# Two-layer relational graph network: single-row transfers on SyncE in layer 2 and on ScalarE in layer 1, and layer 2's root product made in layer 1

## The chip, the core and the metric

The kernel runs on one core of a Trainium2 chip. The time of a run is the core's device time for one execution, in microseconds, and the metric is the median of several runs. The engines of the core work side by side: TensorE (PE in the profile; its weight loads are PEld), VectorE (DVE), ScalarE (ACT), GpSimd (POOL) and SyncE (SP). Each engine takes its instructions in program order, and waits on semaphores for what the others make. A DMA is issued by an instruction in an engine's queue and then runs by itself.

## What is computed

A graph has N = 12500 nodes with 128 features each, and 200000 edges with a source, a destination and one of R = 8 relations. The edges come sorted by destination. Two layers of a relational graph convolution run, each with a residual, and a layer norm ends it. Cut to what matters:

```python
def _rgcn_conv(x, src, dst, et, basis, comp, root, bias):
    W = jnp.einsum('rb,bio->rio', comp, basis)          # 8 matrices 128x128
    xw = jnp.einsum('ni,rio->nro', x, W)
    msgs = xw[src, et]
    seg = dst * N_REL + et
    summed = segment_sum(msgs, seg)
    cnt = segment_sum(ones, seg)
    mean = summed / jnp.maximum(cnt, 1.0)[:, None]
    agg = mean.reshape(N_NODES, N_REL, HIDDEN).sum(axis=1)
    return agg + x @ root + bias

h = x
for l in range(2):
    h = relu(_rgcn_conv(h, src, dst, et, basis[l], comp[l], root[l], bias[l])) + h
return _layernorm(x + h)
```

The part that the change moves is `x @ root + bias` of the second layer, where x is the output h of the first.

## The kernel before

`ordered_path` records every operation in a `Plan`, engine by engine, which afterwards writes out the semaphore waits. So the order on each engine is the order in which the code calls the helpers, and the helpers' lines are what the profile shows: `load` (L701) for every ordinary DMA, `copy` (L704) for ScalarE's copies, `pe`, `vec`, `act` and `pool` for the rest. A DMA issued "on SyncE" or "on ScalarE" stands in that engine's queue among its other instructions.

**Tiles.** The sorted edges are cut into 1563 tiles of 128, and eight tiles make a quad (NQ = 196 quads). Nodes are cut into 98 blocks of 128; a block takes about two quads of edges.

**Rows of the sources.** Each tile needs the 128 rows of its sources, 512 bytes each, at addresses that only the edge list knows. GpSimd gathers them with one indirect DMA per tile (`gather`, L806), into a ring of seven buffers of one quad each (`rows_r`, AHEAD = 5 quads ahead). For some tiles the rows come another way, by single-row transfers: `SINGLES` lists them, as an engine, a layer and a range of tiles. `single_lists` writes the tile's byte offsets to DRAM once. `single_rows` then has the engine load 32 offsets into its registers (L755) and issue one DMA per row (L759), 128 rows in eight chunks of 16, spread over as many steps as lie between two such tiles; every other chunk needs a new register load. The rows land in one of two buffers `hw_`; a tile's last chunk is issued some three quads ahead of its use. Before the change there are 24 such tiles, all of layer 1 and all on SyncE: every 56th from tile 191.

**Layer 1** goes quad by quad, in steps of a loop over o. TensorE forms the means per destination slot and relation from the gathered rows and one-hot tiles of VectorE (`means`, L1364, into two banks `s`); ScalarE copies them to `sT` (`take_means`); TensorE multiplies by the eight relation matrices (`product`, L1396) and puts the result at its node's place (`place`, L1427, with layer 1's root product at L1429); VectorE adds carry and bias, relu and residual (`finish`, L1448, L1452, L1472), which gives a block of hT. From each block `table` (L1495) makes the block's 8 x 128 rows of y = h W_r for layer 2; ScalarE copies them from `pt` or `ct` to `y_row` and stores them to `y_d` in DRAM (`stores`). Tables are made from step TABLE = 50 on, not all of them at once: between steps 94 and 162 (SORT - 2 to SORT + NR + 4) one per step at most, before and after up to two. On ScalarE, `batch(o)` sets the order of a step: the copies that are left from the step before, `ys`, the two `sT` copies, then the stores, then the single rows that ScalarE has, if any.

**Layer 2** gathers rows of `y_d`, which are already multiplied by the relation matrix. Most quads q under 192 that are not in `ROUTED` are summed by slot (`slot_sums`, L2026) from gathered rows; 62 of the quads, every third (7, 10, ... 190), are "routed": TensorE picks their values out of transposed copies of y in SBUF (`pick_rows` L1918, `add_up` L1938, `relate` L1958), with only one gather each for what is left over (`gather_left`). The index lists `lo_d` and `sc_d` of each routed quad, the block hT (`h_d`, `open_block`), x and the output go over SyncE's queue. `place_sums` (L2059) places a quad's sums into the block's accumulator `s`, and in the quad that opens a block adds the root product there (L2063) from the block of `h_d`. `finish` adds the carry of the block before and takes up the next carry with the bias (L1452). The last four quads are added by `add_rows` (L2083).

In layer 2, then, GpSimd has eight gathers per ordinary quad and one per routed quad: 51 in nine quads.

Of the kernel before, what the change touches and what calls it, by code (L numbers as in the profile page):

```python
# [8 lines left out]
F32 = mybir.dt.float32  # L9
# [421 lines left out]
def ordered_path(  # L431
# [80 lines left out]
    RC, RL = 16, 32  # L512
    SINGLES = [("SP", 0, range(191, NQ * Q - 80, 56))]
    SINGLE = {(l, t): (i, k) for i, (_, l, ts) in enumerate(SINGLES) for k, t in enumerate(ts)}
# [16 lines left out]
    w_d = dram.tile([L, R * D, D], F32, name="w_d")  # L531
    h_d = dram.tile([NT, D, P], F32, name="h_d")

    idx = keep([P, B * P], I32, "idx")
# [676 lines left out]
    def rows_of(j):  # L1211
        return min(P, N - j * P)
# [222 lines left out]
    def finish(l, k, apart=False):  # L1435
# [3 lines left out]
        def first_step():  # L1439
            a, ac = acc[k] if apart and k + 1 < NT else acc.pop(k)  # L1440
            emits, reads, cells = [], [ac, ("bias_t", l)], []
            if k >= 0:
                vs[k] = a, ac
            if (l, k) == (1, NT - 1):
                return
            if k >= 0:
                t, c = carry.pop(k)
                emits.append(lambda: nc.vector.tensor_add(a[:, :n], a[:, :n], t[:, :n]))  # L1448
                reads.append(c)
            if k + 1 < NT and not apart:  # L1450
                nt, ncell = carry[k + 1] = carry_r.take()
                emits.append(lambda: nc.vector.tensor_scalar(nt, a[:, P:], bias_t[:, l:l + 1], None, op0=ALU.add))  # L1452
                cells.append(ncell)

            vec(in_turn(emits), reads, cells)
# [29 lines left out]
    def table(j):  # L1485
# [552 lines left out]
    def place_sums(q, k, opens, last):  # L2038
        t, c = pl.pop(q)
        o, oc = ys.pop(q)  # L2040
        a, ac = acc[k]
        root_in = opens and k >= 0
        reads = [c, oc]
        m = NW if q in ROUTED else P
        if root_in:
            ht, hc = hb[k]
            reads += [hc, ("w", 1, R)]
        more = []
# [9 lines left out]
        def emit():  # L2058
            ins = nc.tensor.matmul(a, o[:m], t[:m], start=opens, stop=last and not root_in and not more)  # L2059
            for rows_m, dm_m in more:  # L2060
                ins = nc.tensor.matmul(a, rows_m, dm_m, start=False, stop=last and not root_in)  # L2061
            if root_in:
                ins = nc.tensor.matmul(a[:, :rows_of(k)], w_sb[:, 1, R, :], ht[:, :rows_of(k)], start=False, stop=last)  # L2063
            return ins
# [4 lines left out]
    def add_rows(q, k, opens, last, between_last=None):  # L2069
# [3 lines left out]
        n = in_quad(q)  # L2073
        root_in = opens and k >= 0
        more = []
        if root_in:
            ht, hc = hb[k][0][:, :rows_of(k)], hb[k][1]
            more += [hc, ("w", 1, R)]

        def some(i0, i1):  # L2080
            def emit():
                for i in range(i0, i1):
                    ins = nc.tensor.matmul(a, t[:, i, :], d[:, i, :],  # L2083
                                           start=(opens and i == 0), stop=(last and i == n - 1))
                    if i == 0 and root_in:
                        nc.tensor.matmul(a[:, :rows_of(k)], w_sb[:, 1, R, :], ht, start=False, stop=False)
                return ins

            return emit

        if q == NQ - 2:
            for h in range(2):
                pe(some(4 * h, 4 * h + 4), [c + (h,)] + dc + more, [ac, ("done", 1)])
        elif q == NQ - 1:
# [10 lines left out]
        else:  # L2105
            pe(some(0, n), [c + (0,), c + (1,)] + dc + more, [ac, ("done", 1)])
        plan.mark("PE")
# [207 lines left out]
    for o in range(NG - 3):  # L2315
# [95 lines left out]
    batch(None)  # L2411
    end()
    placed(g - 4)
    product(g - 3)
# [35 lines left out]
    for _, b in halves:  # L2450
        b()

    for q in range(AHEAD):
# [152 lines left out]
```

## Time and profile before

The profile is one execution, taken by the hardware profiler. Its page has, in this order: busy time by engine, the span in 40 slices, DMA queues, the chain of work that ended last, groups of instructions by line, and DMA issues. The views of the trace used beside it are windows (busy time of each engine in a stretch of the span), the timeline of a stretch (start, duration, engine, line, operation, and in brackets the idle time before it with what ended it), and groups by line. A name with q (SPq, ACTq) is the queue of an engine that issues DMAs, whose time isn't counted as busy.

| | |
|---|---|
| runs | 3383.34, 3384.41, 3385.06 us; median 3384.41 |
| the profiled execution's own time | 3385.05 us |
| its span in the trace | 3383.1 us |
| mean granted clock of TensorE | 0.911 |
| moved by DMA | 289.03 MB in 171649 packets, 85 GB/s |
| HBM read / written | 218.35 MB / 65.70 MB |

```profile
## 2 busy tenths in 40 slices
PE   6777667877667777777776739999999999999995
DVE  6665454463367888888333238888888888888884
ACT  1211112222122222222222211111111111111110
POOL 7777777777777777777777777777777777777775
PEclk8999879888888888888988879999999999999997
```

Each digit is a slice of 84.6 us. Layer 1 fills the first 24 slices, the seam between the layers lies in the 24th, and layer 2 fills the rest.

### The profile page before, as it was taken

To read this page: it belongs to the slowest core of one execution; us is meant where nothing else is said; L and a number is where in the kernel's file an instruction comes from. 1 tells how busy PE (TensorE), PEld (TensorE's weight loads), DVE (VectorE), ACT (ScalarE), POOL (GpSimd) and SP (SyncE) were. 2 spreads that over 40 slices of the span, in tenths; PEclk is the share of its full clock that TensorE was granted. 3 is DMA by queue.
4 is the path that set the end of the run, shared out by engine and by line. 5 is a ranking of instruction groups with operands and counts; after the bars stand their busy time and mean duration, and the time that the engine had idled before them with its cause. 6 is when DMAs were issued, how large, how long until landed. Compare 5 with 4: busy or idle time off the path is not lost.

```text
span 3383.1 us, 73915 instructions
## 1 busy us (share of the span) xinstructions
PE 2766.1 (82%) x27537; PEld 2228.2 (66%) x27537; DVE 2270.8 (67%) x6302; ACT 644.9 (19%) x1627; POOL 2547.9 (75%) x2677
## 2 busy tenths in 40 slices
PE   6777667877667777777776739999999999999995
PEld 4565565656566666766565627777777777777774
DVE  6665454463367888888333238888888888888884
ACT  1211112222122222222222211111111111111110
POOL 7777777777777777777777777777777777777775
PEclk8999879888888888888988879999999999999997
DMA  4242223443322232222333232233223322333222
GB/s 138 56 59 64 57 77 113 132 130 95 89 82 81 75 89 76 82 77 82 115 105 89 88 101 73 72 84 85 78 78 84 84 78 78 84 85 82 78 78 61
DMA packets 171649, 289.03 MB, mean 85 GB/s; under 512 B 66163, under 2 KB 102813, under 8 KB 171285
## 3 DMA queue, kind: packets, MB, share of 16 engines
q0 software_dynamic: 85408, 175.09, 20.3%
q1 hardware_dynamic: 47146, 50.19, 5.0%
q10 hardware_dynamic: 38731, 58.99, 4.9%
q8 instruction: 218, 3.57, 0.5%
q14 instruction: 146, 1.20, 0.1%
HBM read 218.35 MB, written 65.70 MB: 84 GB/s over the span
## 4 chain that ended last, share of the span: by engine, by line
PE 43%; POOL 40%; issue 13%; DVE 2%; DMA 2%; ACT 1%; POOLq 0%; ACTq 0%; SPq 0%; DVEq 0%
POOL rows L806 40%; PE pt L1918 11%; PE y L1938 9%; PE po L1938 7%; PE po L1958 3%; PE s L2059 3%; PE ct L2026 2%; PE s L1364 2%; PE y L1396 1%; DMA rows<-in_x_dram,idx 1%; PE s L2061 1%; DVE dm L1270 1%; PE s L2063 1%; DVE arena L999 1%; PE pt L1495 0%
## 5 line engine op out<-in xcount | busy, mean ns | idle before, releaser
L806 POOL DMA_INDIRECT rows<-in_x_dram,idx x1539 | 1476.8, 960 | 471.3 <-issue 463.5
L806 POOL DMA_INDIRECT rows<-y_d,idy x1067 | 1010.4, 947 | 325.1 <-issue 316.6
L1364 PE MATMUL s<-dm,rows 128*128 128x128 f32 x3078 | 531.6, 344 | 379.6 <-DMA rows<-in_x_dram,idx 351.8
L1364 PEld LDWEIGHTS s<-dm,rows 128*128 128x128 f32 x3078 | 495.2, 252 | 441.1 <-issue 228.1
L1270 DVE TENSOR_SCALAR dm<-cols,kr,w 128x128 f32<-128x128 f16 x1563 | 525.1, 400 | 194.7 <-PE pt L1495 54.8
L1396 PE MATMUL y<-w_sb,sT 128*128 128x128 f32 x3136 | 438.6, 299 | 46.4 <-ACT sT L704 46.4
L1396 PEld LDWEIGHTS y<-w_sb,sT 128*128 128x128 f32 x3136 | 424.6, 217 | 56.4 <-ACT sT L704 55.2
L1918 PE MATMUL pt<-arena,dm 128*32 128x128 f32 x12152 | 391.3, 275 | 2.8 <-DVE dm L1868 2.1
L704 ACT ACTIVATE sT<-s 128x512 f32<-128x512 f32 x391 | 212.3, 594 | 824.8 <-PE s L1364 824.8
L1918 PEld LDWEIGHTS pt<-arena,dm 128*32 128x32 f32 x12152 | 324.6, 110 | 55.2 <-issue 43.0
L1938 PE MATMUL y<-arena,dm 128*128 128x304 f32 x620 | 229.6, 452 | 35.1 <-DVE arena L1885 35.1
L1229 DVE TENSOR_SCALAR sT<-cols,kr,w 128x32 f32<-128x32 f16 x1040 | 238.1, 300 | 7.4 <-PE s L2063 7.3
L1868 DVE TENSOR_TENSOR dm<-arena,cols 128x768 f32<-128x768 f16 x248 | 231.3, 933 | 4.1 <-DMA dm<-sc_d 3.7
L1448 DVE TENSOR_TENSOR po<-po,carry 128x128 f32<-128x128 f32 x98 | 28.8, 294 | 296.9 <-PE pt L1495 104.2
L1938 PE MATMUL po<-arena,dm 128*128 128x304 f32 x620 | 210.3, 421 | 0.0
L704 ACT ACTIVATE dm<-pt 128x256 f32<-128x256 f32 x248 | 95.4, 385 | 578.2 <-PE pt L1918 533.6
L1495 PE MATMUL pt<-w_sb,arena 128*128 128x512 f32 (+1 forms) x326 | 174.5, 618 | 26.3 <-ACT y_row L704 14.9
L704 ACT ACTIVATE y_row<-pt 128x512 f32<-128x512 f32 x165 | 98.5, 597 | 417.8 <-PE pt L1495 153.3
L1938 PEld LDWEIGHTS y<-arena,dm 128*128 128x128 f32 x620 | 102.9, 189 | 88.4 <-DVE arena L1885 35.3
L1885 DVE TENSOR_SCALAR arena<-cols,comp_sb 128x608 f32<-128x608 f16 x155 | 134.9, 902 | 36.1 <-DMA arena<-y_d,arena 36.0
L1938 PEld LDWEIGHTS po<-arena,dm 128*128 128x128 f32 x620 | 118.4, 191 | 41.3 <-issue 0.7
L1885 DVE TENSOR_SCALAR arena<-cols,sel 128x608 f32<-128x608 f16 x155 | 134.8, 902 | 0.0
(327 smaller groups left out, 3583.5 us busy)
## 6 DMA issues: line engine op xcount, KB each, us to landing
hw_SP<-in_x_dram SPq DMA_DIRECT2D x3072, 0.5 KB
y_d<-y_row ACTq DMA_DIRECT2D x96, 512.0 KB
rows<-in_x_dram,idx POOLq DMA_INDIRECT x1539
rows<-y_d,idy POOLq DMA_INDIRECT x1067
arena<-lo_d SPq DMA_DIRECT2D x62, 256.0 KB
x_g<-in_x_dram SPq DMA_DIRECT2D x24, 512.0 KB
h_d<-arena ACTq DMA_DIRECT2D x96, 64.0 KB
out_dram<-x_g SPq DMA_DIRECT2D x12, 512.0 KB
```

The lines of the kernel that those rows point to most:

```text
L704: act(lambda: nc.scalar.activation(out_t, in_t, AF.Copy), reads, writes)
L806: ins.append(nc.gpsimd.indirect_dma_start(out=t[:, i - q * Q, :], out_offset=None, in_=table_t, in_offset=bass.IndirectOffsetOnAxis(ap=ids ...
L1229: vec(in_turn([lambda i=i: nc.vector.tensor_scalar(t[:, i, :], cols[:, :2 * K], kr[:, i0 + i:i0 + i + 1], w[:, i0 + i:i0 + i + 1], op0=ALU ...
L1270: emits.append(lambda i=i: nc.vector.tensor_scalar(t[:, i - q * Q, :wide], cols[:, :wide], ids[:, i:i + 1], w[:, i:i + 1], op0=ALU.is_equa ...
L1364: last = nc.tensor.matmul(s_b[i // 4][0][:, i % 4, :], t[:, i, :] if one is None else one[0], d[:, i, :], start=True, stop=True)
L1396: last = nc.tensor.matmul(y[:m], t[:, r, :nt, :].rearrange("p t k -> p (t k)"), w_sb[:, 0, r, :], start=(r == 0), stop=(r == R - 1))
L1495: pe(lambda: nc.tensor.matmul(hb[:n].rearrange("p r d -> p (r d)"), hT[:, j * P:j * P + n], w_sb[:, 1, k * H:(k + 1) * H, :].rearrange("p ...
L1868: emits = [lambda: nc.vector.tensor_tensor(o[:, :3 * n].rearrange("p (j c) -> p j c", j=3), bits[:, None, u * n:(u + 1) * n].to_broadcast( ...
L1885: vec(lambda v=v, o=o: nc.vector.tensor_scalar(o, segs_p, sg[:, v:v + 1], sg[:, NTL + v:NTL + v + 1], op0=ALU.is_equal, op1=ALU.mult), ["n ...
L1918: last = nc.tensor.matmul(b[k * CAP:(k + 1) * CAP, x, :], o[:n, c:c + CAP], hT[:n, j * P:(j + 1) * P], start=jj == 0, stop=jj == SIZE[g] - 1)
L1938: last = nc.tensor.matmul(b.rearrange("p t d -> p (t d)")[:, :SEG], g[:, x * P:(x + 1) * P], o[:, k * SEG:(k + 1) * SEG], start=v == 0, st ...
L1958: pe(in_turn([lambda r=r: nc.tensor.matmul(b[:NW, 0, :], t_s[:, r * NW:(r + 1) * NW], w_sb[:, 1, r, :], start=r == 0, stop=r == R - 1) for ...
```

## The change

Three things are changed.

1. `SINGLES` gets two entries. SyncE brings 21 tiles of layer 2 (every 72nd from tile 95, so one in nine quads, none of them in a routed quad), and ScalarE 12 tiles of layer 1 (every 104th from tile 244, one in 13 quads). GpSimd no longer gathers these 33 tiles. The address list of each entry is made by `single_lists` at the step that `LISTED` gives for its layer.
2. A new function `rooting(k)` makes layer 2's root product for block k in layer 1, one step or more after the block's hT is there: one matmul of TensorE into a free part of the `y` bank, one ScalarE instruction that adds the bias and puts it in one of two buffers `hr`, and a store to `hr_d` on ScalarE's queue.
3. In layer 2 `open_block` loads `hr_d[k]` beside `h_d[k]`, on SyncE; `finish` makes the carry of block k+1 by adding `hr` in place of the bias; the root matmul goes from `place_sums` and `add_rows`. The last block, 97, keeps its own root product.

```diff
-    SINGLES = [("SP", 0, range(191, NQ * Q - 80, 56))]
+    SINGLES = [("SP", 0, range(191, NQ * Q - 80, 56)), ("SP", 1, range(95, (NQ - 4) * Q, 72)), ("ACT", 0, range(244, NQ * Q - 80, 104))]
...
+    hr_d = dram.tile([NT, D, P], F32, name="hr_d")
...
+    hr_r = Ring(const, 2, [P, P], F32, "hr")
+    hr, rooted = {}, []
...
             if k + 1 < NT and not apart:
                 nt, ncell = carry[k + 1] = carry_r.take()
-                emits.append(lambda: nc.vector.tensor_scalar(nt, a[:, P:], bias_t[:, l:l + 1], None, op0=ALU.add))
+                if l == 1 and k + 1 < NT - 1:
+                    rt, rc = hr.pop(k + 1)
+                    emits.append(lambda: nc.vector.tensor_add(nt, a[:, P:], rt))
+                    reads.append(rc)
+                else:
+                    emits.append(lambda: nc.vector.tensor_scalar(nt, a[:, P:], bias_t[:, l:l + 1], None, op0=ALU.add))
...
+    def rooting(k):
+        n = rows_of(k)
+        b, bc = y_full[0][:, 1, :n], y_full[1]
+        t, c = hr_r.take()
+        pe(lambda: nc.tensor.matmul(b, w_sb[:, 1, R, :], hT[:, k * P:k * P + n], start=True, stop=True),
+           [("h", k), ("w", 1, R)], [bc])
+        plan.mark("PE")
+        act(lambda: nc.scalar.activation(t[:, :n], b, AF.Identity, bias=bias_t[:, 1:2]), [bc, ("bias_t", 1)], [c])
+        plan.mark("ACT")
+        stores.append(lambda: load(hr_d[k][:, :n], t[:, :n], [c], [("hr_d", k)], "ACT"))
...
         load(t[:, :n], h_d[k][:, :n], [("h_d", k)], new(c))
         hb[k] = t, c
+        if k < NT - 1:
+            t, c = hr[k] = hr_r.take()
+            load(t[:, :n], hr_d[k][:, :n], [("hr_d", k)], [c])
...
         def emit():
-            ins = nc.tensor.matmul(a, o[:m], t[:m], start=opens, stop=last and not root_in and not more)
+            ins = nc.tensor.matmul(a, o[:m], t[:m], start=opens, stop=last and not more)
             for rows_m, dm_m in more:
-                ins = nc.tensor.matmul(a, rows_m, dm_m, start=False, stop=last and not root_in)
-            if root_in:
-                ins = nc.tensor.matmul(a[:, :rows_of(k)], w_sb[:, 1, R, :], ht[:, :rows_of(k)], start=False, stop=last)
+                ins = nc.tensor.matmul(a, rows_m, dm_m, start=False, stop=last)
             return ins
...
             if k >= 0:
                 stores.append(lambda k=k: load(h_d[k][:, :rows_of(k)], hT[:, k * P:k * P + rows_of(k)], [("h", k)],
                                                [("h_d", k)], "ACT"))
+                if k < NT - 1:
+                    rooted.append(k)
                 tables.extend(table(k))
...
         for step in behind:
             pe(*step)
             plan.mark("PE")
         behind.clear()
+        if rooted:
+            rooting(rooted.pop(0))
         if len(tables) > 4 and (TABLE <= o < SORT - 2 or o >= SORT + NR + 4):
```

How this changes the order on ScalarE, in a step of layer 1 that makes two tables. Before (the number behind a name is a buffer's, and `y_row` stands for the rows of y that go to `y_d`):

```order
L704 ACTIVATE ys_120<-y 128x128
L704 ACTIVATE sT_113<-s_136 128x4x8x16
L704 ACTIVATE sT_113<-s_137 128x4x8x16
L701 DMA y_d<-y_row_127 128x1024
L704 ACTIVATE y_row_128<-pt 128x512
L704 ACTIVATE y_row_127<-pt 128x512
L704 ACTIVATE y_row_127<-ct 128x512
L704 ACTIVATE ys_121<-y 128x128
```

and a like step of the changed kernel that has a chunk of a single-row tile (`hw_ACT`) and a root product (`hr`); lines are those of the changed kernel:

```order
L708 ACTIVATE ys_119<-y 128x128
L708 ACTIVATE sT_114<-s_137 128x4x8x16
L708 ACTIVATE sT_114<-s_138 128x4x8x16
L705 DMA y_d<-y_row_128 128x1024
L759 TENSOR_LOAD off_d_165
L763 DMA hw_ACT_158<-in_x_dram 1x512 x16
L1535 ACTIVATE hr_154<-y,bias_t 128x128
L708 ACTIVATE y_row_129<-pt 128x512
L708 ACTIVATE y_row_128<-pt 128x512
L708 ACTIVATE y_row_128<-ct 128x512
L708 ACTIVATE ys_120<-y 128x128
```

The register load, the sixteen row transfers and the root product's copy now stand between the store and the three copies out of `pt` and `ct`.

On SyncE, in layer 2, the loads of the routed quads' lists (`lo_d`, `sc_d`) and of the blocks (`h_d`) were alone:

```order
L701 DMA arena<-lo_d 128x1024
L701 DMA id_k<-h_d 128x128
L701 DMA dm<-sc_d 16x128
L701 DMA id_r<-h_d 128x128
L701 DMA arena<-lo_d 128x1024
L701 DMA jmp<-h_d 128x128
L701 DMA dm<-sc_d 16x128
```

In the changed kernel the same stretch of the queue reads:

```order
L705 DMA arena<-lo_d 128x1024
L705 DMA id_k<-h_d 128x128
L705 DMA hr_155<-hr_d 128x128
L759 TENSOR_LOAD off_d_164
L763 DMA hw_SP_157<-y_d 1x512 x32
L705 DMA dm<-sc_d 16x128
L705 DMA id_r<-h_d 128x128
L705 DMA hr_154<-hr_d 128x128
L759 TENSOR_LOAD off_d_164
L763 DMA hw_SP_157<-y_d 1x512 x16
L705 DMA arena<-lo_d 128x1024
L763 DMA hw_SP_157<-y_d 1x512 x16
```

Each block load is followed by one of `hr_d`, and chunks of 16 rows, with a register load before every other one, stand between the block loads and the lists.

More of the change, by code (lines that the diff above doesn't have):

```diff
@@ L2041, in place_sums @@
         a, ac = acc[k]
-        root_in = opens and k >= 0
         reads = [c, oc]
         m = NW if q in ROUTED else P
-        if root_in:
-            ht, hc = hb[k]
-            reads += [hc, ("w", 1, R)]
         more = []
@@ L2058, in emit @@
         def emit():
-            ins = nc.tensor.matmul(a, o[:m], t[:m], start=opens, stop=last and not root_in and not more)
+            ins = nc.tensor.matmul(a, o[:m], t[:m], start=opens, stop=last and not more)
             for rows_m, dm_m in more:
-                ins = nc.tensor.matmul(a, rows_m, dm_m, start=False, stop=last and not root_in)
-            if root_in:
-                ins = nc.tensor.matmul(a[:, :rows_of(k)], w_sb[:, 1, R, :], ht[:, :rows_of(k)], start=False, stop=last)
+                ins = nc.tensor.matmul(a, rows_m, dm_m, start=False, stop=last)
             return ins
@@ L2073, in add_rows @@
         n = in_quad(q)
[L2074 to L2078, printed above, removed]
         def some(i0, i1):
@@ L2084, in emit @@
                                            start=(opens and i == 0), stop=(last and i == n - 1))
-                    if i == 0 and root_in:
-                        nc.tensor.matmul(a[:, :rows_of(k)], w_sb[:, 1, R, :], ht, start=False, stop=False)
                 return ins
@@ L2092, in add_rows @@
             for h in range(2):
-                pe(some(4 * h, 4 * h + 4), [c + (h,)] + dc + more, [ac, ("done", 1)])
+                pe(some(4 * h, 4 * h + 4), [c + (h,)] + dc, [ac, ("done", 1)])
         elif q == NQ - 1:
@@ L2105, in add_rows @@
         else:
-            pe(some(0, n), [c + (0,), c + (1,)] + dc + more, [ac, ("done", 1)])
+            pe(some(0, n), [c + (0,), c + (1,)] + dc, [ac, ("done", 1)])
         plan.mark("PE")
@@ L2412, in ordered_path @@
     end()
+    while rooted:
+        rooting(rooted.pop(0))
     placed(g - 4)
@@ L2451, in ordered_path @@
         b()
+    while rooted:
+        rooting(rooted.pop(0))
+    rooting(NT - 2)
+    for step in stores:
+        step()
+    stores.clear()
     for q in range(AHEAD):
```

## The prediction

> **What bounds the kernel now.** I read the page's head, its chain and its costliest groups first, then the stages as windows.
>
> ```profile
> span 3383.1 us, 73915 instructions
> PE 2766.1 (82%) x27537; PEld 2228.2 (66%) x27537; DVE 2270.8 (67%) x6302; ACT 644.9 (19%) x1627; POOL 2547.9 (75%) x2677
> PE 43%; POOL 40%; issue 13%; DVE 2%; DMA 2%; ACT 1%; POOLq 0%; ACTq 0%; SPq 0%; DVEq 0%
> L806 POOL DMA_INDIRECT rows<-in_x_dram,idx x1539 | 1476.8, 960 | 471.3 <-issue 463.5
> L806 POOL DMA_INDIRECT rows<-y_d,idy x1067 | 1010.4, 947 | 325.1 <-issue 316.6
> ```
>
> GpSimd looks like a 75% engine and is a full one. Its gathers take 0.945 us, each behind 0.3 us of issue, and nearly none of its idle time has another releaser: one gather every 1.25 us, from the first microsecond to the last stage, without a stop between the layers.
>
> ```profile
> core 0: us, PE busy (x) PEld busy (x) DVE busy (x) ACT busy (x) POOL busy (x), PEclk, DMA share, GB/s
> 560.00:960.00 400.00, 298.21 (x1700) 241.84 (x1701) 179.99 (x547) 100.91 (x206) 303.32 (x318) 0.88 0.36 110
> 1600.00:1780.00 180.00, 132.98 (x753) 106.40 (x751) 65.92 (x203) 47.06 (x99) 136.08 (x145) 0.90 0.35 108
> 2030.00:3300.00 1270.00, 1264.51 (x17659) 965.64 (x17658) 1085.03 (x2768) 193.33 (x561) 960.39 (x1017) 1.00 0.29 80
> ```
>
> In layer 1 (the first two stages shown) TensorE and ScalarE have room and GpSimd has none. In layer 2 TensorE is full as well. Which of the two sets the end there shows in its last stretch:
>
> ```profile
> L2063 PE MATMUL s<-id_r,w_sb x64: 272/275/422, 2040.1 to 3324.2; 128*128 128x128 f32 x64
> 3333.56 1.10 PE L2026 MATMUL ct<-rows,sT 128*32 128x128 f32 x16 [8.90 <-DMA rows<-y_d,idy]
> 3342.45 6.72 PE L2083 MATMUL s<-dm,rows 128*128 128x256 f32 x16 [4.50 <-DMA rows<-y_d,idy]
> ```
>
> The first row times the blocks: block 1 opens at 2040.1 and block 94 at 3324.2, so 93 blocks take 1284.1 us, 13.81 per block of two quads, 62.1 per nine quads. In nine quads GpSimd makes 6 x 8 + 3 = 51 gathers, 63.75 us. TensorE starts layer 2 late, catches up by 1.6 us in nine quads, and at 3333 waits 8.9 us for rows: GpSimd's queue sets the end, TensorE comes a hair behind it.
>
> **The change part by part.** *Gathers.* 12 leave GpSimd in layer 1 and 21 in layer 2: 33 x 1.25 = 41.2 us, 15.0 and 26.2. That is the gain if everything else keeps up. TensorE would: the root product is two instructions, and sixteen such take 1.8 us back to back (1006.06, below), so a product is 0.22 us, 21 us over the 95 that leave layer 2's blocks, or 1.0 per nine quads. In layer 1 that work meets an engine with 26% idle.
>
> ```profile
> L1448 DVE TENSOR_TENSOR po<-po,carry 128x128 f32<-128x128 f32 x98 | 28.8, 294 | 296.9 <-PE pt L1495 104.2
> L1452 DVE TENSOR_SCALAR carry<-po,bias_t 128x128 f32<-128x128 f32 x97 | 33.1, 341 | 0.0
> ```
>
> The carry turns from a scalar form of 0.34 into a tensor-tensor add, of which a like one takes 0.29: nothing.
>
> *What pays for the gathers* is the queue of another engine, and for that I read the transfers of before.
>
> ```profile
> L755 SPq TENSOR_LOAD <-off_d x96: 3512/3756/4675, 190.3 to 1758.5; - x96
> 640.67 21.45 SPq L759 DMA_DIRECT2D hw_SP<-in_x_dram  x52
> 1011.92 7.98 SPq L759 DMA_DIRECT2D hw_SP<-in_x_dram  x25
> 2502.64 0.32 SPq L701 DMA_DIRECT2D arena<-lo_d  x1
> 2503.00 0.43 SPq L701 DMA_DIRECT2D id_k<-h_d  x1
> ```
>
> A row costs 7.98/25 = 0.32 us of its engine's queue in a clean stretch. The 52 rows of 21.45 us have one register load of 3.76 among them: 0.34. A tile of 128 rows has four loads: at 0.34, which I take as the longer stretch, 15.0 + 43.5 = 58.6 us; at 0.32 and the shortest load 55.
>
> *SyncE in layer 2.* It has nine quads per tile. In them stand, beside the tile, 3 loads of `lo_d`, 3 of `sc_d`, 4.5 of `h_d`, the 4.5 new ones of `hr_d`, and one of x or out: 16 at 0.32 to 0.43, 5.1 to 6.9. Together **64.5 us, against 62.5 that GpSimd then needs (50 gathers) and 61.1 of TensorE**. SyncE becomes the slowest. Behind its rows, in order, wait the block loads, for which VectorE's carry and residual wait. Against the pace of before that is 2.4 us per nine quads, and 93 blocks are 20.7 times nine: +49. A tile's last chunk is issued three quads ahead of its use, so 20.7 us of lag cost nothing: +28. At the end TensorE no longer waits 8.9 us for GpSimd, which is ahead by then: -9. Layer 2: **+19**. The bounds: at 55 + 5.1 = 60.1 SyncE is hidden and the layer gains 1.25 us per nine quads on GpSimd's pace, about -26; with none of the lag forgiven +49.
>
> *ScalarE in layer 1.* A tile goes in eight chunks of 16 rows, each after the step's `sT` copies, and every other one behind a register load: 5.4 or 9.2 us in 8 of 13 steps. Here is a step of the first stage with tables:
>
> ```profile
> 649.79 2.05 PE L1364 MATMUL s<-dm,rows 128*128 128x128 f32 x16 [2.65 <-DMA rows<-in_x_dram,idx]
> 651.88 0.60 ACT L704 ACTIVATE sT<-s 128x512 f32<-128x512 f32 x1 [3.45 <-PE s L1364]
> 651.88 0.33 ACTq L701 DMA_DIRECT2D y_d<-y_row  x1
> 652.37 0.59 ACT L704 ACTIVATE sT<-s 128x512 f32<-128x512 f32 x1
> 654.52 0.60 ACT L704 ACTIVATE y_row<-pt 128x512 f32<-128x512 f32 x1 [1.56 <-PE pt L1495]
> 655.17 1.12 PE L1495 MATMUL pt<-w_sb,arena 128*128 128x512 f32 x2 [0.26 <-ACT y_row L704]
> 656.14 1.02 PE L1495 MATMUL ct<-w_sb,arena 128*128 128x512 f32 x2
> 657.20 0.60 ACT L704 ACTIVATE y_row<-pt 128x512 f32<-128x512 f32 x1 [2.07 <-PE ct L1495]
> 658.75 1.83 PE L1364 MATMUL s<-dm,rows 128*128 128x128 f32 x14 [1.59 <-DMA rows<-in_x_dram,idx]
> 660.84 0.60 ACT L704 ACTIVATE sT<-s 128x512 f32<-128x512 f32 x1 [2.39 <-PE s L1364]
> 658.17 0.28 ACT L704 ACTIVATE ys<-y 128x128 f32<-128x128 f32 x1
> 1000.99 0.44 ACTq L701 DMA_DIRECT2D lo_d<-arena  x1
> ```
>
> ScalarE frees `pt` at 654.52, and TensorE's second table waits for it. The queue hands out the store at 651.88, so the chunk would run from 652.2 to 657.6, or to 661.4 with a load; with the `hr` copy (0.28, as `ys`) that `y_row` starts 3.4 or 7.2 us late, and all of TensorE behind it with it: table, second table in `ct`, the next means. Without a chunk and with rows at hand, TensorE could go on at 657.1, and the next `sT` would come 2.1 us after (658.75 to 660.84): a step of 7.3. With one it is 10.7 or 14.5. Thirteen steps: 5 x 7.3 + 4 x 10.7 + 4 x 14.5 = 137, and 1.5 for seven root products, **against 13 x 10.0 - 1.25 = 128.8 of GpSimd**. To that comes the clock:
>
> ```profile
> 1006.06 1.80 PE L1364 MATMUL s<-dm,rows 128*128 128x128 f32 x14 [1.22 <-ACT arena L704]
> 1016.56 3.75 PE L1364 MATMUL s<-dm,rows 128*128 128x128 f32 x16 [4.36 <-DMA rows<-in_x_dram,idx]
> ```
>
> After a wait of 4.4 us the means take 3.75 instead of 1.8 to 2.05, and the granted clock of the stage is 0.88. A TensorE that waits 3 to 7 us for ScalarE pays about 1.8 us more: in the four loaded steps and half the others, 11 us. The excess is 21 us in 13 quads. The Trainium skill's TensorE: Matmul & The Clock Gate (HAM oscillation) says that an idle stretch of more than some 3.4 us puts the array back to half clock; the two rows agree. Without the clock the excess would be 10.
>
> Tables stand in 560 to 960 and from 1600 until the last chunk near 1750, some 53 quads or 4.1 times thirteen: 86 us of lag. (Between them, and before, steps have one table or none; I take their lag as constant.) The ring of seven row tiles lets GpSimd run on for five and a half quads, 55 us; the rest, 31 us, it stands still. With the 15.0 gained, layer 1: **+16**. Bounds: -15 with no stall; with rows at 0.44, the longer of ScalarE's own issues (`lo_d`), 13 us more in each thirteen, +69. That the lag left drains before the layer ends I take from the 7.3 us step: 2.7 us a quad over the 22 quads behind the last chunk.
>
> *The layers' seam.* The last root product stands behind the last tables, so `y_d` is not later, and GpSimd ends first there:
>
> ```profile
> 1949.39 0.95 POOL L806 DMA_INDIRECT rows<-in_x_dram,idx  x1 [0.30 <-issue]
> 2026.40 1.86 DVE L1885 TENSOR_SCALAR arena<-cols,comp_sb 128x608 f32<-128x608 f16 x2 [36.02 <-DMA arena<-y_d,arena]
> ```
>
> The layer's last gather is out at 1949, and VectorE's first selection behind the seam waits 36.0 us for rows until 2026: a shift of layer 1 goes through whole, and the last products, 22 quads of 0.22 late at most, cost nothing. The address lists add two small loads: nothing.
>
> **The sum**, against the profiled execution's own time, 3385.05 us (span 3383.1, 1.95 around it; the median of the three runs, 3384.41, is 0.6 less): 3385 + 16 + 19 = **3420**.
>
> **The rivals.** *Both queues keep up.* Mechanism: the chunk lies in the time that ScalarE stands idle (in 560 to 960 it is busy 101 of 400 us), TensorE catches up in the five free steps, and SyncE at 0.32 a row is inside 62.5. It decides at a mean excess of zero: thirteen steps under 128.8 us, a ScalarE row of 0.25 or a second table not held. Then GpSimd's 33 gathers are the whole effect: 3385 - 41 = 3344. The Trainium skill's Perfetto Trace Analysis (DMA Optimizations) has it so: where descriptor generation is what keeps an engine solid, balance the DMAs over the engines that can issue. GpSimd here is such an engine, and the trace agrees about it; that the others have the room is what the 58.6 us per tile speak against. *SyncE keeps up, ScalarE doesn't:* 16 - 26, 3375. *ScalarE keeps up, SyncE doesn't:* -15 + 19, 3389. *Both worse:* rows at 0.44 on ScalarE, or the steps between the tables lagging too: 69 + 19, 3473.
>
> **How the numbers follow.** The forecast of 3420 (3395 to 3445) 0.42; both keep up, 0.14; only SyncE, 0.15; only ScalarE, 0.12; both worse, 0.17. The range, 3345 to 3490, leaves out the lower half of the first rival (0.07) and the upper part of the last (0.08). Within 0.2% (about what a measurement of this kernel can tell from no change) means 3378 to 3391: faster by more has the first rival and most of the second, 0.25; within, the rest of it and half of the third, 0.10; slower 0.65.
>
> **What would show it.** GpSimd's gathers of layer 1 with releasers on TensorE, some 30 us, and its last one at about 1965 instead of 1949; TensorE waiting for `y_row` copies by more than 3 us in 560 to 960, at a clock under 0.88; SyncE's issues without a gap in layer 2, blocks at 14.2 us instead of 13.8, and waits of slot sums for `hw_SP` or of VectorE for `hr`. Wrong it is if GpSimd never waits, or if blocks come at 13.6.

## The result and the profile after

| | median | runs | |
|---|---|---|---|
| before | 3383.95 us | 5, 3383.15 to 3385.06 | |
| changed | 3480.24 us | 5, 3473.26 to 3487.11 | ratio 1.0287, interval 1.0271 to 1.0303 |

The change costs 96 us. The forecast was 3420, 36 us slower, with a range up to 3490. The direction and the range held, the size did not. The profiled execution took 3477.2 us.

The page's head and its chain of work, with the two groups of gathers:

```profile
span 3475.3 us, 83036 instructions
PE 2732.8 (79%) x27537; PEld 2164.6 (62%) x27537; DVE 2264.0 (65%) x6304; ACT 674.1 (19%) x1724; POOL 2508.3 (72%) x2644
PE 34%; SPq 17%; ACTq 16%; DVE 11%; issue 10%; POOL 5%; DMA 4%; ACT 4%; DVEq 0%; POOLq 0%
L810 POOL DMA_INDIRECT rows<-in_x_dram,idx x1527 | 1457.4, 954 | 529.7 <-issue 454.2 <-PE s L1368 69.3 <-DMA arena<-in_dst_dram 2.3
L810 POOL DMA_INDIRECT rows<-y_d,idy x1046 | 990.3, 947 | 391.0 <-issue 306.2 <-PE ct L2049 75.9 <-PE s L2080 3.4
```

The chain has moved: GpSimd held 40% of it and now 5%, and two queues of DMA issues, SyncE's and ScalarE's, hold 33%. GpSimd now stops, 69 us in layer 1 and 76 us in layer 2, both times for a row buffer that TensorE has not yet released.

Where the 92 us of span come from is read from the first and last start of the gathers, here before and after (views of the tile `rows`):

```profile
L806 POOL DMA_INDIRECT rows<-in_x_dram,idx x1539: 940/945/1986, 4.6 to 1949.4; - x193
L806 POOL DMA_INDIRECT rows<-y_d,idy x1067: 940/945/1817, 1950.6 to 3363.7; - x178
```

```profile
L810 POOL DMA_INDIRECT rows<-in_x_dram,idx x1527: 938/944/1883, 4.5 to 1988.3; - x191
L810 POOL DMA_INDIRECT rows<-y_d,idy x1046: 938/944/2599, 1989.6 to 3448.4; - x175
```

Layer 1 ends its gathers at 1988.3 instead of 1949.4: **+38.9**. Layer 2's take 1458.8 us instead of 1413.1: +45.7. The stretch behind the last gather, 19.4 before, is 26.9 now: +7.5. So **layer 2 and the end cost 53 us**.

**Layer 1.** The queue and the engines in a step before any table is made (timelines of ScalarE and of TensorE):

```profile
224.47 1.08 ACT L708 ACTIVATE sT<-s 128x512 f32<-128x512 f32 x2
228.67 5.34 ACTq L763 DMA_DIRECT2D hw_ACT<-in_x_dram  x16
234.05 0.28 ACT L708 ACTIVATE ys<-y 128x128 f32<-128x128 f32 x1 [8.50 <-issue]
235.21 0.37 ACT L1535 ACTIVATE hr<-y,bias_t 128x128 f32<-128x128 f32 x1 [0.88 <-PE y L1532]
```

```profile
234.38 0.80 PE L1532 MATMUL y<-arena,w_sb 128*128 128x128 f32 x2 [4.99 <-ACT ys L708]
235.82 3.41 PE L1368 MATMUL s<-dm,rows 128*128 128x128 f32 x16
239.06 1.95 PE L1400 MATMUL y<-w_sb,sT 128*128 128x128 f32 x16
```

```profile
core 0: us, PE busy (x), PEclk, DMA share, GB/s
229.40:232.00 2.60, 0.00 (x0) 1.00 0.20 52
232.10:238.80 6.70, 4.42 (x18) 0.50 0.23 61
```

`ys`, the copy out of the `y` bank, stands behind a register load and the chunk: ScalarE computes nothing for 8.5 us ahead of it. The root product writes a part of the same bank, which the plan tracks as one piece, so it waits 5.0 us for that copy, and everything of TensorE behind it waits too: place, and the next means. Those then take 3.41 us where the sixteen products behind them take 1.95: the granted clock is 0.50 from 232.1 to 238.8 (last view), and 1.00 before and behind that stretch. The Trainium skill's TensorE: Matmul & The Clock Gate (HAM oscillation) warns of idle gaps of more than some 3.4 us, behind which the next matmuls start at the throttled clock. The trace agrees for this wait of 5.0 us; here the lower clock set in 2.6 us after TensorE's last matmul. Such waits add up (waits of TensorE from 200 to 560 us, before and after):

```profile
PE s L1364 <- DMA rows<-in_x_dram,idx: 50.5, 24, 4.1
PE y L1396 <- ACT sT L704: 30.8, 27, 1.2
```

```profile
PE y L1400 <- ACT sT L708: 41.0, 15, 7.4
PE y L1532 <- ACT ys L708: 35.0, 12, 7.2
PE pt L961 <- ACT arena L708: 34.6, 4, 11.5
```

How late TensorE is when the first table begins shows in the first start of `table`, here before and after:

```profile
L1495 PE MATMUL pt<-w_sb,arena x326: 592/592/1222, 517.9 to 1962.9; 128*128 128x512 f32 x162, 128*84 128x512 f32 x1
L1504 PE MATMUL pt<-w_sb,arena x326: 592/595/1223, 553.4 to 2001.6; 128*128 128x512 f32 x162, 128*84 128x512 f32 x1
```

It is 35.5 us late there, before any table is made.

**Layer 2.** SyncE's rows, a stretch of its queue, and the last chunk of the first tile and of the last:

```profile
L763 SPq DMA_DIRECT2D hw_SP<-y_d x2688: 227/228/724, 2029.3 to 3430.5; - x192
2599.69 0.36 SPq L705 DMA_DIRECT2D jmp<-h_d  x1
2600.10 0.42 SPq L705 DMA_DIRECT2D hr<-hr_d  x1
2600.62 5.11 SPq L763 DMA_DIRECT2D hw_SP<-y_d  x16
2605.83 0.32 SPq L705 DMA_DIRECT2D dm<-sc_d  x1
2609.91 5.09 SPq L763 DMA_DIRECT2D hw_SP<-y_d  x16
2106.18 5.12 SPq L763 DMA_DIRECT2D hw_SP<-y_d  x16
3425.66 5.12 SPq L763 DMA_DIRECT2D hw_SP<-y_d  x16
```

The waits of VectorE and SyncE from 2126 to 3396, SyncE's longest from 2029 to 2126, and its longest before the change, from 2030 to 3300:

```profile
DVE s L1452 <- DMA hr<-hr_d: 188.6, 57, 6.5
SPq L705 <- PE pt L1941: 1.6, 5, 0.6
SPq L705 <- PE po L1919: 21.6, 1, 21.6
SPq L701 <- PE po L1896: 552.9, 59, 44.6
```

From 2126 on SyncE never rests: its longest sum of waits is 1.6 us of 1270 (the hole before 2609.91 is a register load). Before the change one releaser alone held it 553 us. The rows of 21 tiles take from 2029.3 to 3430.5. Among them is one stop of 21.6 us, in the first tile; from the last chunk of the first tile to that of the last, 20 tiles take 1319.5 us, **66.0 us each**, for nine quads. An `hr` load takes 0.52 us of the queue (2600.10 to 2600.62). VectorE's add waits for it in 57 blocks. At the end it is the same queue (timelines of TensorE and of GpSimd):

```profile
3432.21 0.87 PE L2049 MATMUL ct<-rows,sT 128*32 128x128 f32 x11 [17.22 <-DMA hw_SP<-y_d]
3407.15 0.94 POOL L810 DMA_INDIRECT rows<-y_d,idy  x1 [43.26 <-PE ct L2049]
```

TensorE waits 17 us for the last tile that SyncE brings, whose last row is issued at 3430.5. It waits for no gathered rows any more: GpSimd had been so far ahead that it stood still for 43 us for a buffer, so that the 26 us which 21 gathers less save are lost in waiting.

### The profile page after: what moved, and what is told of

The parts are those of the page before. It is cut to its first block, busy times and chain, and to the rows that moved or that the text cites. A ratio compares the mean times of both kernels' runs of the same rounds, so it can differ in the third digit from the quotient of the medians.

```text
span 3475.3 us, 83036 instructions
## 1 busy us (share of the span) xinstructions
PE 2732.8 (79%) x27537; PEld 2164.6 (62%) x27537; DVE 2264.0 (65%) x6304; ACT 674.1 (19%) x1724; POOL 2508.3 (72%) x2644
## 4 chain that ended last, share of the span: by engine, by line
PE 34%; SPq 17%; ACTq 16%; DVE 11%; issue 10%; POOL 5%; DMA 4%; ACT 4%; DVEq 0%; POOLq 0%
ACTq L763 11%; SPq L763 10%; PE s L1368 7%; SPq L759 5%; POOL rows L810 5%; PE y L1400 5%; PE pt L1941 4%; ACTq L759 4%; PE y L1961 3%; PE pt L1504 3%; PE po L1961 3%; SPq L705 2%; DVE dm L1274 2%; DMA hr<-hr_d 1%; ACT sT L708 1%
## 5 line engine op out<-in xcount | busy, mean ns | idle before, releaser
L810 POOL DMA_INDIRECT rows<-in_x_dram,idx x1527 | 1457.4, 954 | 529.7 <-issue 454.2
L810 POOL DMA_INDIRECT rows<-y_d,idy x1046 | 990.3, 947 | 391.0 <-issue 306.2
L1274 DVE TENSOR_SCALAR dm<-cols,kr,w 128x128 f32<-128x128 f16 x1563 | 526.2, 403 | 130.8 <-PE ct L1504 62.1
L1368 PEld LDWEIGHTS s<-dm,rows 128*128 128x128 f32 x3054 | 407.4, 211 | 78.3 <-issue 73.6
L1368 PE MATMUL s<-dm,rows 128*128 128x128 f32 x3054 | 422.1, 296 | 35.7 <-DMA hw_SP<-in_x_dram 17.7
L1941 PE MATMUL pt<-arena,dm 128*32 128x128 f32 x12152 | 404.6, 281 | 57.0 <-DVE dm L1891 36.9
L1941 PEld LDWEIGHTS pt<-arena,dm 128*32 128x32 f32 x12152 | 336.1, 112 | 123.5 <-issue 116.6
L1504 PE MATMUL pt<-w_sb,arena 128*128 128x512 f32 (+1 forms) x326 | 197.1, 690 | 129.2 <-ACT y_row L708 116.5
L1961 PE MATMUL y<-arena,dm 128*128 128x304 f32 x620 | 230.9, 454 | 35.6 <-DVE arena L1908 35.3
L1452 DVE TENSOR_TENSOR s<-s,carry 128x128 f32<-128x128 f32 x97 | 28.8, 297 | 233.0 <-DMA hr<-hr_d 210.6
L1504 PEld LDWEIGHTS pt<-w_sb,arena 128*128 128x128 f32 (+1 forms) x326 | 58.5, 213 | 146.7 <-ACT y_row L708 129.2
```

Source lines behind the costliest of these rows:

```text
L810: ins.append(nc.gpsimd.indirect_dma_start(out=t[:, i - q * Q, :], out_offset=None, in_=table_t, in_offset=bass.IndirectOffsetOnAxis(ap=ids ...
L1274: emits.append(lambda i=i: nc.vector.tensor_scalar(t[:, i - q * Q, :wide], cols[:, :wide], ids[:, i:i + 1], w[:, i:i + 1], op0=ALU.is_equa ...
L1368: last = nc.tensor.matmul(s_b[i // 4][0][:, i % 4, :], t[:, i, :] if one is None else one[0], d[:, i, :], start=True, stop=True)
L1504: pe(lambda: nc.tensor.matmul(hb[:n].rearrange("p r d -> p (r d)"), hT[:, j * P:j * P + n], w_sb[:, 1, k * H:(k + 1) * H, :].rearrange("p ...
L1941: last = nc.tensor.matmul(b[k * CAP:(k + 1) * CAP, x, :], o[:n, c:c + CAP], hT[:n, j * P:(j + 1) * P], start=jj == 0, stop=jj == SIZE[g] - 1)
L1961: last = nc.tensor.matmul(b.rearrange("p t d -> p (t d)")[:, :SEG], g[:, x * P:(x + 1) * P], o[:, k * SEG:(k + 1) * SEG], start=v == 0, st ...
```

## The experiments

The change has three parts, and the trace shows two queues that hold up TensorE; the theory was that a part costs only where its queue or its bank is shared. The first four runs take the parts singly and in one pair. Ratios are to the kernel before on the same chip; "lag" is the start of VectorE's add of block 28 (quad 57), in the timeline, less that of before (622.8).

**Root product alone.** The changed kernel with before's list:

```diff
-    SINGLES = [("SP", 0, ...), ("SP", 1, range(95, (NQ - 4) * Q, 72)), ("ACT", 0, range(244, NQ * Q - 80, 104))]
+    SINGLES = [("SP", 0, range(191, NQ * Q - 80, 56))]
```

> Only the root product is moved; no tile changes its engine. Theory (queue time: SyncE's queue is full in layer 2 with the single rows, and the hr loads are only a share of it): hr_d adds 4.5 loads of 0.50 us per nine quads to a queue that is mostly idle without the rows, GpSimd still makes 51 gathers per nine quads and sets the end: 3384, 3380 to 3390. Rival (hand-over: the load of hr itself comes late, with a ring of two and its way through DRAM, since VectorE waited 211 us for hr in the changed kernel, 2.2 per block): blocks slower without any single rows too, 3400 to 3450, with VectorE waiting for hr.

3378.64 us, 0.9993 (0.9984 to 1.0003): nothing. The hand-over of `hr` costs nothing by itself.

**SyncE's 21 tiles alone.** The kernel before, with `("SP", 1, range(95, (NQ - 4) * Q, 72))` added.

> Only the 21 tiles of layer 2 go to SyncE; root product and bias as before. Theory (queue time): the changed kernel's nine quads hold SyncE 65.8 us, 2.3 of them for hr; 63.5 are left, against 62.5 of GpSimd and 62.1 of TensorE: SyncE is still the slowest, blocks near 14.1 us, layer 2 longer by 10 to 30 us: 3395 to 3415, and TensorE or VectorE waits for loads from SyncE. Rival (hand-over of hr): nothing waits for hr now, TensorE sets the pace at 62.1 and its wait of 8.9 us at the end goes: 3375.

3384.05 us, 1.0011 (1.0001 to 1.0020): neither. SyncE is full here too, with 63.5 us for a tile (from last chunk to last chunk, as above), but TensorE keeps its 62.1 up to block 56. Then it waits for late block loads (`h_d`, 20 us in all) and lags by 8 us at block 91; GpSimd, 28 us ahead, loses all but 4 of that waiting for a buffer.

**ScalarE's 12 tiles alone.** The kernel before, with `("ACT", 0, range(244, NQ * Q - 80, 104))` added.

> Only the 12 tiles of layer 1 go to ScalarE; root product as before. Theory (coupling: before step 50 only the root product's matmul, which shares the y bank, has TensorE wait for the ys copy that stands behind the chunk): TensorE does not fall behind before the tables; in the two stages with tables it does, by about 30 us in the first, which the ring of seven buffers takes up: GpSimd stops little, 3369 to 3385. Rival (the chunk alone does it): TensorE some 50 us behind at quad 56 as in the changed kernel, GpSimd stops 35 to 70 us in layer 1, 3410 to 3425.

3380.32 us, 1.0006 (0.9993 to 1.0019). The first table starts 6.6 us late, nearly as the theory has it. The lag is 29 us at block 28 and 60 at its peak, at block 38; the last gather is at 1943.1, 6 us early.

**Root product and ScalarE's 12 tiles.** The changed kernel without SyncE's 21.

> Root product moved and 12 tiles of layer 1 on ScalarE; layer 2 gathers as before. Theory (coupling): layer 1 as in the changed kernel, its last gather 39 us later, then layer 2 at GpSimd's pace of 63.75 per nine quads: 3384 + 39 = 3423, 3415 to 3430. Rival (no coupling): the sum of what root alone and ScalarE alone cost against before.

3421.16 us, 1.0119 (1.0103 to 1.0136). First table 41 us late, lag 65 us, last gather at 1990.8. Each part alone is free, the two together cost 40. The waits of TensorE from 200 to 560, with ScalarE's tiles alone and with the root product beside them:

```profile
PE y L1396 <- ACT sT L704: 56.9, 26, 6.4
PE pt L957 <- ACT arena L704: 34.9, 4, 11.3
PE pt L1495 <- ACT y_row L704: 13.1, 3, 7.8
```

```profile
PE y L1400 <- ACT sT L708: 53.8, 15, 19.5
PE y L1532 <- ACT ys L708: 35.3, 12, 7.4
PE pt L961 <- ACT arena L708: 34.6, 4, 11.4
```

The row that is new, 35.3, is of the size of the difference of the two lags, 36. (The window holds tables in the first run, which is earlier there. Over the same work, from block 5 to block 28, all waits for ScalarE are 140 us without the root product and 171 with it.)

**Four kernels on two chips on which the kernel before takes 1.48 times as long.** The root product with SyncE's tiles; root and ScalarE with the root product's place moved (the edit is shown below); the root product with every 96th tile on SyncE; and the root product with SyncE's 21 tiles and the `hr` loads on ScalarE.

> The change without ScalarE's 12 tiles. Theory (SyncE's queue in layer 2 holds 65.8 us per nine quads with the hr loads, 63.5 without, and only the first is more than TensorE and GpSimd can bear): the same 59 us that stand between the changed kernel and root plus ScalarE: 3384 + 57 = 3440, 3430 to 3450, blocks at 14.6 us. Rival (the lag that layer 1 brings in makes layer 2 worse): with no lag at the seam 3400 to 3420.

> Root product and ScalarE's 12 tiles, with the root product's place in the order moved: in batch(o), behind the copies and ahead of ys and sT, so that neither its matmul nor its copy stands behind a chunk of the step. Theory (coupling by that place): TensorE no longer waits for ys ahead of the root product, lag at quad 56 near 29 us as with ScalarE's tiles alone, layer 1's last gather 0 to 8 us earlier than before: 3376 to 3386. Rival (any root product beside the chunks costs it, by TensorE's and ScalarE's added work): 3410 to 3421 again.

> Root product, and on SyncE every 96th tile of layer 2 (16 tiles) instead of every 72nd. Theory (queue time): in twelve quads SyncE has 58.4 + 7.4 x 12/9 = 68.3 us of work against 83.75 of GpSimd and 81.5 of TensorE, so it is hidden: 16 x 1.25 = 20 us gained, 3364, up to 3372 if TensorE ends late. Rival (a chunk of 5 to 9 us ahead of an hr load is late by itself, at any mean load): VectorE still waits for hr, 3385 to 3410.

> Root product and 21 tiles on SyncE, with the hr loads of layer 2 issued by ScalarE. Theory (queue time): SyncE is back at 63.5 per nine quads, 1.0 over GpSimd's 62.5, so 20 us behind after the layer, most of which three quads of lead take up: 26 gained, 0 to 15 given back: 3358 to 3373. Rival (the hand-over of hr through DRAM and two buffers is what VectorE waits for, whichever queue issues it): VectorE waits for hr as before, 3400 to 3440.

On the first of these chips the kernel before took 5005.92 us; the same four, run again, met another on which it took 5017.62.

> The change without ScalarE's 12 tiles, again, on a chip at its usual clock. Theory (SyncE's queue in layer 2 holds 65.8 us per nine quads with the hr loads, 63.5 without, and only the first is more than TensorE and GpSimd can bear): the same 59 us that stand between the changed kernel and root plus ScalarE: 3384 + 57 = 3440, 3430 to 3450, blocks at 14.6 us. Rival (the lag that layer 1 brings in makes layer 2 worse): with no lag at the seam 3400 to 3420.

> Root product and ScalarE's 12 tiles, with the root product's place in the order moved, again: in batch(o), behind the copies and ahead of ys and sT. Theory (coupling by that place): TensorE no longer waits for ys ahead of the root product, lag at quad 56 near 29 us as with ScalarE's tiles alone, layer 1's last gather 0 to 8 us earlier than before: 3376 to 3386. Rival (any root product beside the chunks costs it, by TensorE's and ScalarE's added work): 3410 to 3421 again.

> Root product, and on SyncE every 96th tile of layer 2 (16 tiles) instead of every 72nd, again. Theory (queue time): in twelve quads SyncE has 58.4 + 7.4 x 12/9 = 68.3 us of work against 83.75 of GpSimd and 81.5 of TensorE, so it is hidden: 16 x 1.25 = 20 us gained, 3364, up to 3372 if TensorE ends late. Rival (a chunk of 5 to 9 us ahead of an hr load is late by itself, at any mean load): VectorE still waits for hr, 3385 to 3410.

> Root product and 21 tiles on SyncE, with the hr loads of layer 2 issued by ScalarE, again. Theory (queue time): SyncE is back at 63.5 per nine quads, 1.0 over GpSimd's 62.5, so 20 us behind after the layer, most of which three quads of lead take up: 26 gained, 0 to 15 given back: 3358 to 3373. Rival (the hand-over of hr through DRAM and two buffers is what VectorE waits for, whichever queue issues it): VectorE waits for hr as before, 3400 to 3440.

The ratios there were 1.0246 and 1.0231, 1.0189 and 1.0198, 1.0122 and 1.0073, 1.0248 and 1.0229. TensorE's mean granted clock was 0.79 to 0.81, against 0.90 to 0.92 elsewhere, and a part of its idle time has no releaser in the trace. These eight runs answer none of their questions; what slows those chips was not looked into. So the root product with SyncE's 21 tiles, without ScalarE's, has no time at the usual clock.

**The whole change, with two edits.** The root product's place, from behind the product to `batch(o)`, behind the left-over copies and ahead of `ys` and `sT`; and the `hr` loads on ScalarE's queue:

```diff
         copies.clear()
+        if rooted and o is not None:
+            rooting(rooted.pop(0))
         for g in late_y:
...
         behind.clear()
-        if rooted:
-            rooting(rooted.pop(0))
...
-            load(t[:, :n], hr_d[k][:, :n], [("hr_d", k)], [c])
+            load(t[:, :n], hr_d[k][:, :n], [("hr_d", k)], [c], "ACT")
```

> The whole change with two edits: the root product stands in batch(o), behind the copies and ahead of ys and sT, and in layer 2 the hr loads are issued by ScalarE instead of SyncE. Layer 1, theory (coupling by its place behind the chunk): last gather 0 to 8 us earlier than before; rival (root product beside the chunks costs it anywhere): some 40 us later. Layer 2, theory (SyncE's queue time): 63.5 per nine quads instead of 65.8, blocks at 13.8 to 14.1 us, 11 to 26 us gained; rival (hand-over of hr): VectorE waits some 200 us for hr, blocks near 14.6, 57 us lost. Both theories right: 3352 to 3372.

3400.48 us, 1.0059 (1.0042 to 1.0076). Layer 1: first table 9.6 us late, lag 39, last gather at 1961.5, 12 us late; between the two expectations. Layer 2: SyncE is still full (its waits are 2 us at most for any releaser), with 63.7 us for a tile, and VectorE no longer waits for `hr`; the first gather comes 12.1 us late, the last 11.4, and nothing is gained. So the `hr` loads' queue time was the loss, 97 x 0.5 = 48.5 us: the rows last 1355 us here and 1401 in the changed kernel. The gain that I expected from what was left did not come: at 63.7 us SyncE takes as long for nine quads as GpSimd's 51 gathers did before, 63.75. One rival stays untested: the lag that layer 1 brings in, 39 us in the changed kernel and 12 here, might make SyncE's queue cost more. By itself such a lag costs layer 2 nothing: root product and ScalarE's tiles bring in 41 us, and layer 2's gathers take 1412.0 us there.

**The same place, 16 tiles on SyncE.** Every 96th tile instead of every 72nd, `hr` on SyncE.

> The whole change with the root product in batch(o) as in the run beside it, hr on SyncE, and every 96th tile of layer 2 (16) instead of every 72nd (21). Layer 1 as in the run beside it. Layer 2, theory (queue time): 68.3 us of SyncE in twelve quads of 83.75, hidden: 20 us gained; rival (a chunk of 5 to 9 us ahead of an hr load makes it late at any mean load): VectorE waits for hr, nothing gained or up to 25 us lost. Both theories right: 3356 to 3370.

3374.02 us, 0.9979 (0.9969 to 0.9988). The gathers of this run:

```profile
L810 POOL DMA_INDIRECT rows<-in_x_dram,idx x1527: 938/944/1886, 4.6 to 1966.5; - x191
L810 POOL DMA_INDIRECT rows<-y_d,idy x1051: 940/944/2727, 1967.7 to 3360.5; - x176
SPq L705 <- DVE dm L1897: 144.4, 52, 5.7
```

Layer 2's gathers take 1392.8 us, 20.3 less than before: 16 x 1.25 = 20.0. SyncE rests again (the last row: 144 us from 2126 to 3280 for one releaser), and a chunk ahead of an `hr` load costs nothing. Layer 1 is 17 us late, its first table 12.6.

**What is left, and what pays.** Root product and 16 tiles; 16 tiles on the kernel before; 16 tiles and ScalarE's 12 on the kernel before; and the kernel of the section above (moved place, 12 tiles on ScalarE, 16 on SyncE) with the root product's copy on VectorE:

```diff
-        act(lambda: nc.scalar.activation(t[:, :n], b, AF.Identity, bias=bias_t[:, 1:2]), [bc, ("bias_t", 1)], [c])
-        plan.mark("ACT")
+        vec(lambda: nc.vector.tensor_scalar(t[:, :n], b, bias_t[:, 1:2], None, op0=ALU.add), [bc, ("bias_t", 1)], [c])
+        plan.mark("DVE")
```

> Root product as in the change, 16 tiles of layer 2 on SyncE (every 96th), none on ScalarE; again, on a chip at its usual clock. Theory (a queue with room costs nothing): layer 1 as with the root product alone, layer 2 16 x 1.25 = 20 us shorter as in g2: 3361, 3356 to 3366, faster than before. Rival (TensorE's or SyncE's lateness eats it): 3370 to 3384.

> 16 tiles of layer 2 on SyncE, root product and bias as before. Theory (GpSimd sets layer 2's pace as long as it is slower than TensorE): per twelve quads GpSimd has 83.75 us and TensorE 62.1 x 12/9 = 82.8, so all 20 us are gained without the root product's move: 3361 to 3366. Rival (TensorE, which starts layer 2 late, becomes the end without the 21 us that the move takes off it): 9 us gained, 3372 to 3376.

> 16 tiles of layer 2 on SyncE and the 12 tiles of layer 1 on ScalarE, root product and bias as before. Theory: layer 1's last gather 6 us earlier as with ScalarE's tiles alone, and layer 2 as in h2: 6 us under h2, 3355 to 3370. Rival (TensorE, late by ScalarE's chunks, can't use it): same as h2 or above.

> As g2 (root product ahead of the chunk, ScalarE's 12 tiles, 16 tiles on SyncE), with the root product's copy and bias made by VectorE instead of ScalarE. Theory (what is left of layer 1's loss is the copy's place on ScalarE, which the y bank waits for): last gather of layer 1 6 us early to 5 us late, 3350 to 3364. Rival (it is TensorE's own added work and colder clock): 12 to 17 us late as in g2, 3370 to 3377.

| | us | ratio | gathers of layer 1 end | of layer 2 |
|---|---|---|---|---|
| root, 16 on SyncE | **3356.41** | 0.9920 (0.9904 to 0.9937) | 1942.4 | 1943.6 to 3336.6 |
| 16 on SyncE | 3368.07 | 0.9957 (0.9940 to 0.9973) | 1950.4 | 1951.7 to 3351.8 |
| 16 on SyncE, 12 on ScalarE | 3369.50 | 0.9967 (0.9957 to 0.9976) | 1952.1 | 1953.3 to 3352.6 |
| moved place, 16 on SyncE, 12 on ScalarE, copy on VectorE | 3514.20 | 1.0396 (1.0378 to 1.0413) | 2089.9 | 2091.1 to 3483.5 |

The first is the fastest kernel of the study, 25 us under before's 3381.83 beside it, and faster than both kernels. Its layer 2 gains the 20 us whole (1393.0). Its layer 1 is 7 us early because the same 1539 gathers were busy 1469.6 us instead of 1476.8, which no part of the change explains. On the two slow chips this kernel lost 0.7 and 1.2%. Its chain is GpSimd's again:

```profile
POOL 43%; PE 40%; issue 14%; DMA 1%; ACT 0%; DVE 0%; POOLq 0%; ACTq 0%
```

Without the root product's move 7 of the 20 us don't come: TensorE is the bound, its last blocks stand where they stood before (block 91 is 1.0 us late), and GpSimd, 18 us ahead, waits for buffers. So the move pays as soon as GpSimd comes near TensorE's pace. ScalarE's 12 tiles add nothing to that.

The copy on VectorE fails both expectations: layer 1's last gather is 140 us late. VectorE now waits for the root product's matmul (waits from 200 to 560):

```profile
DVE hr L1535 <- PE y L1532: 146.0, 18, 21.6
```

So it says nothing about the 12 to 17 us that are left in layer 1 with the root product ahead of the chunk; those stay open. A part of them may be no effect at all: ScalarE's 12 tiles without the root product ended layer 1 at 1943.1 in one run and, with SyncE's 16 tiles of layer 2, at 1952.1 in another, 9 us apart.

## Why the prediction was right in sign and wrong in size

- **What bounds the kernel before** held: GpSimd sets the pace, with TensorE a hair behind. 16 gathers less are 20.3 us less when the other queues have room and the root product is gone from layer 2, and 13 when it is not.
- **Layer 1: +16 forecast, +38.9 measured.** The step that failed is "Between them, and before, steps have one table or none; I take their lag as constant". The lag before the first table, put at nothing, is 35.5 us. The tables' part was near the size forecast: the lag grows by 60 more to its peak of 95 at block 38, and by 17 in the second stage with tables, 77 against the forecast 86. But with 35.5 us of the ring's 55 already used up (5.5 quads of 10 us), GpSimd stood still 69.3 us for TensorE's buffers, and not 31. I had priced the root product by its length, 0.22 us, and its ScalarE copy by 0.28 (0.37 measured), and had not asked what its matmul waits for. It shares the bank `y`, whose reader `ys` is queued behind a chunk: 35 us of waits in twelve steps. The runs show it: the first table is 6.6 us late with ScalarE's tiles alone, 1.7 with the root product alone, 41 with both, and 9.6 and 12.6 when the root product stands ahead of the chunk. At the end of layer 1 the moved place takes 22 to 29 of the 39 to 41 us back; the rest arises in the stages with tables and stays open.
- **Layer 2: +19 forecast, 53 measured.** The mechanism held: SyncE the slowest, its issues without a gap, VectorE waiting for `hr`. The term that was mis-sized is SyncE's time for nine quads, 64.5 forecast, 66.0 measured. The tile was priced right (58.6; its rows and register loads take 58.2 in the trace), the other 16 loads were not: 5.9 forecast, some 7.5 measured. They were priced at 0.32 to 0.43, as their issue lasts; from one issue to the next an `hr` or `h_d` load takes 0.41 to 0.52. Against TensorE's 62.1, the pace of before, that makes 3.9 x 20.7 = 81 us instead of 49. The lead of three quads was to forgive 20.7, which leaves 60; TensorE's lag grew by 60 (39 at the first block, 99 at block 91, by VectorE's add). The same sum gives 12 us for the 63.7 of the run with `hr` on ScalarE and 8 for the 63.5 of SyncE's tiles alone; the lags grew by 12 and 10 there.
- **The end: -9 forecast.** From 99 at block 91 the lag comes to 92 at the end, -7. That the numbers lie near each other is luck: TensorE no longer waits for gathered rows, as forecast, but that wait was 20.7 us before (from 3297 on) and not 8.9, and it waits 17 us for SyncE's last tile, which I had not counted.
- **The rivals.** The one in which both queues keep up was to decide at 62.5 us for SyncE; in layer 2 the run with 16 tiles is that case. The time measured, 3480, is near that of *Both worse*, 3473, but not by its sum: ScalarE's rows took 0.33 us and not 0.44, layer 1 cost 39 us and not 69, layer 2 53 and not 19. The Trainium skill's Perfetto Trace Analysis (DMA Optimizations) advises to balance DMAs over the engines that can issue, where making descriptors is the bottleneck. These runs agree as far as the engine's queue has room, 16 tiles on SyncE (20.3 us gained), and no further: 21 with the `hr` loads lost 53.
- I had added the parts up as if they were independent; they are not. Alone the three measured -2, +3 and -1 us by their medians, root product and ScalarE's tiles together +40, all three +96.

## What to carry to other kernels

Price a transfer in the issuing engine's queue from one issue to the next, add up everything in that queue over a period, and compare the sum with the slowest engine's: a part that is free below the limit costs its full time above it. Before a burst of issues goes into the queue of an engine that also copies TensorE's results out of their banks, list what stands behind it and which matmuls write those banks; a short matmul put into a shared bank inherits the wait. Run the parts of a change alone and in pairs.

## What the runs showed of the hardware

- A single-row transfer of 512 bytes takes 0.32 to 0.33 us of SyncE's and of ScalarE's queue alike (16 in 5.11 and 5.34 us), and a load of 32 registers 3.77 and 3.83 (medians, below): 58 us for a tile of 128 rows with its four register loads, against 1.25 of GpSimd.

```profile
L759 SPq TENSOR_LOAD <-off_d x180: 3539/3770/11112, 195.5 to 3415.5; - x180
L759 ACTq TENSOR_LOAD <-off_d x48: 3607/3834/4601, 198.3 to 1776.2; - x48
```

- Two chips ran the kernel before 1.48 times as long as the others, at a mean granted clock near 0.80, and changed the sign of an edit: what wins 0.8% elsewhere lost 0.7 to 1.2% there.
